# A four-layer fp32 transformer on one core: edge tokens in the first query block, more places for background pieces, and the last FFN kept for the tail

## The chip, the cores and the metric

The kernel runs on one core of a Trainium2 chip. A core has five engines with their own instruction queues: TensorE (PE, matmuls and transposes), VectorE (DVE), ScalarE (ACT), GpSimd (POOL) and SyncE (SP, which here issues the DMAs). The metric is the device time of one execution in microseconds; the time before is the median of three runs.

## The reference, cut to what matters

One sequence of 2048 tokens of width 128 goes through four layers, each an attention and an FFN with a residual sum around either (`x = x + f(layernorm(x))`), all in fp32:

- Layer 0: attention with 16 heads of width 8; FFN with an exact GELU.
- Layer 1: full attention with 16 heads of width 64 over all 2048 keys; FFN with 384 hidden columns and a SiLU gate.
- Layer 2: attention of every token to itself and its two neighbours in a ring (token 0 and token 2047 are neighbours); FFN with one of eight experts.
- Layer 3: a memory that is updated in 32 chunks of 64 tokens, each of which needs the state that the chunk before left; FFN with eight routed experts and a shared one, 176 hidden columns each.

```python
idx = jnp.stack([(i - 1) % s, i, (i + 1) % s], axis=1)      # layer 2: the ring
...
for c0 in range(0, S, CHUNK):                                # layer 3: 32 chunks in series
    g = _grad_fn(W_state, k[:, sl], v[:, sl]) * GRAD_SCALE
    ...
    (S_state, W_state), Wtraj = jax.lax.scan(step, (S_state, W_state), xs)
```

## The kernel before, in words

The kernel has three phases. Layer 0 runs first (0 to 906 us in the trace). Then layer 1's attention (`l1_attn`, 906 to 2595 us), with everything behind it as background work. Then the tail (`drain`, 2595 to 2999 us), in which the rest of that background work is done.

**Layer 1's attention.** The 2048 queries are cut into blocks of 512, 384, 512, 384 and 256 (`QB`: start, tokens, columns). A unit is one block with one pair of heads, so a block has eight units and the phase 40. A unit has 16 key steps of 128 keys. A key step issues four passes of score matmuls for the two heads (`ops`: high and low parts of keys and queries, and the negative row maximum), two exponentials on ACT, a few matmuls that look for the maxima of a later unit (`max_upto`, reduced by DVE into `mx`), the sums of the exponentials (`do_sum`, mostly on POOL) and the value matmuls of the step before (`do_pv`). After a unit, `u_end` divides by the sums, through DRAM, and after every second unit `stage_wo` multiplies by the output weights. With a block's last unit its tokens are added to `xs`, and `("x", qb)` is emitted: the block is ready for what follows.

**Edge tokens.** Background work runs in blocks of 256 tokens. Layer 2's attention of such a block (`stage_b`) needs a neighbour's keys and values on both sides. So that it needn't wait for the next query block, the attention of a few tokens (`EXTRA`) is computed as extra columns of one query block: tokens 1280, 1792 and 2047, in the second block, which has 388 columns instead of 384. `stage_m` takes these tokens through layer 1's FFN and writes their keys and values into `edge`. `stage_b` waits for `"m"`, and for the following block of 256 unless that block's first token is an extra one.

**Background.** For each block of 256 the stages are `stage_a` (layer 1's FFN), `stage_a2` (layer 2's projections), `stage_b`, `stage_b2` (layer 2's FFN), then for each 128 tokens `stage_c`, two times `chunk` (the recurrence of layer 3) and `stage_d`, and then `stage_g` (the router of the last FFN), `stage_e0`, the lanes `s_lane` (13 tiles of hidden columns for each block, 104 in all) and `stage_e1`. Each is a generator which yields wherever it would have to wait for another engine. What is yielded says what the next piece needs: a whole number asks for so many PSUM banks, `"T"` says that the piece has matmuls, a float is a delay.

**The planner.** The order on PE, DVE, ACT and POOL is written out when the program is built. `note` keeps an estimated clock for each engine. `fill` lets background pieces in: it goes through the helpers and parts in their order of priority and takes the first that `may` go, by its estimated ready time, by how far ACT and DVE are behind (`backlog`, `low`) and by free banks (`leave` banks are left alone), until the estimated PE clock has moved by a limit. With `only="t"` it takes only pieces that need no bank and aren't marked as having matmuls; since these leave the PE clock where it is, such a call takes all that are ready. In a key step of layer 1 there are two calls of `fill`, after the exponentials and maxima and after the value matmuls. The estimate can charge 0.12 us whenever the shape of the weights' tile on PE changes (`in0`); layer 0 is planned with that, layer 1 and the tail without.

PSUM has eight banks: three for scores (`st`), five (`mx`) for maxima, the value product and the background. In the tail all eight serve the background, and five more lanes take part.

Of the kernel before, what the change touches and what calls it, by code (L numbers as in the profile page):

```python
# [30 lines left out]
ATANH = (1.0000000039388743, 0.3333315796754013, 0.20012426861749952, 0.13980709417165652, 0.14087328632693624)  # L31
T = dict(lead0=22, more0=4, mgap=0.4, pvq=2, lim0=0.5, fq=(3,), pl=-0.5, pr=1.0, tlow=2, tback=3, late=0.3, pvp="mx", mxp="mx", ex=(1280, 1792, 2047), low=1, lows='ge', keep=1, leave=2, pvn=1, sp=0, rdy=40., eu=2, qg=(22, 16, 10), em=2, el=6, sem=0.2, same=1.2, tsame=3.0, order="hdmBbAaEcCeg", ps=dict(st=3, mx=5), dma=2.3, slack=0.1, lim=0.3, backlog=2.5, lead=(10, 8, 6), pp=7, dve=(14, 15), qp=(1, 1), lanes=2, xl=5,
         QB=[(0, 512, 512), (512, 384, 388), (896, 512, 512), (1408, 384, 384), (1792, 256, 256)])

# [36 lines left out]
def body(ctx: ExitStack, tc: tile.TileContext, x, pa, pb, pc, pi, pd, pr, pr0, pe, pw, out):  # L71
# [122 lines left out]
    class Part:  # L194
# [24 lines left out]
        def step(self):  # L219
            piece[0] = clk["T"]  # L220
            r = next(self.gen, "end")
            self.same = r == "same"
            self.ready = 0.0 if self.same else piece[0] + (r if type(r) is float else 0.0)
            self.pe = r == "T"
            self.banks = r if type(r) is int else 0
            self.seen = len(emitted) if r is False else -1
            if r == "end":
                emitted.add(self.key)
            return r != "end"
# [139 lines left out]
    xnd = dram.tile([128, S], F32, name="xnd")  # L369

    QB = T["QB"]
    EXTRA = T['ex']
    units = [(qb, p) for qb in range(len(QB)) for p in range(NP1)]
    qhh, qfs, kmx, mx1 = {}, {}, {}, {}

    qx = [mid.tile([128, 8], F32R, name=f"qx{i}") for i in range(2)]
    xq = {}

    def u_loadx(qb):
        t0, tn, n = QB[qb]  # L380
        xq[qb] = l1x.tile([128, 512], F32, name="xq", tag="xq", bufs=2)
        if n != tn:
            ge.memset(xq[qb][:, tn:n], 0.0)
            for i, t in enumerate(EXTRA):
                sy.dma_start(xq[qb][:, tn + i:tn + i + 1], xnd[:, t:t + 1])
        sy.dma_start(xq[qb][:, :tn], xnd[:, t0:t0 + tn])

    def u_qprep(u):
        qb, p = units[u]
        if qb not in xq:  # L390
            u_loadx(qb)
        n = QB[qb][2]
        yield 1
        ps = mi()
        mm(ps[:, :n], C("wq", p * 128, 128), xq[qb][:, :n])
        yield
        qf = l1x.tile([128, 512], F32, name="qf", tag="qf")
        se.activation(qf[:, :n], ps[:, :n], AF.Identity, bias=bq8[:, p:p + 1], scale=0.125)
        rel(ps)
        yield  # L400
        qhh[u] = l1q.tile([128, 512], F32R, name="qh", tag="qh")
        se.copy(qhh[u][:, :n], qf[:, :n])
        yield
        qfs[u] = qf
        tn, n = QB[qb][1:]
        if n > tn:
            for e in range(2):
                r = slice(64 * e, 64 * e + 64)
                se.copy(qx[u % 2][r, 4 * e:4 * e + n - tn], qf[r, tn:n])

# [14 lines left out]
    def u_max(u, i):  # L425

        qb, p = units[u]
        tn, n = QB[qb][1:]
        per = nmax(u) // 4
        c, r = divmod(i, per)  # L430
        qt, e = divmod(r, 2)
        if i == 0:
            mx1[u] = sm.tile([128, 2, 4, 4], F32, name="mx1", tag="mx1")
        if 128 * qt == tn:
            ps = amx()
            mm(ps[0:8], qx[u % 2], kmx[(u, c)])
            ve.tensor_reduce(mx1[u][0:8, 0, 3, c:c + 1], ps[0:8], AX.X, ALU.max)
            rel(ps)
            return 1
        pss = [amx() for _ in range(2)]  # L440
        for e in range(2):
            rows = slice(64 * e, 64 * e + 64)
            mm(pss[e], qhh[u][rows, qt * 128:(qt + 1) * 128], kmx[(u, c)][rows, :], par=e and 0.02)
        for e in range(2):
            ve.tensor_reduce(mx1[u][:, e, qt, c:c + 1], pss[e], AX.X, ALU.max)
            rel(pss[e])
        return 2

    def u_maxend(u):
# [6 lines left out]
        if n > tn:  # L456
            ve.tensor_reduce(m[0:8, 0, 3:4], mx[0:8, 0, 3, :], AX.X, ALU.max)
        yield 1
        t = mi()
        if n > tn:  # L460
            te.transpose(t[0:1, 256:264], m[0:8, 0, 3:4], ident[0:8, 0:8])
        for e in range(2):
# [4 lines left out]
        if n > tn:  # L467
            for e in range(2):
                se.mul(mbt[u % 2][64 * e:64 * e + 1, tn:n], t[0:1, 256 + 4 * e:256 + 4 * e + n - tn], -1.0)
        rel(t)  # L470
# [480 lines left out]
    psum_pools(**T["ps"])  # L951
    in0[0] = False
    leave[0] = T["leave"]
# [69 lines left out]
    def stage_wo(qb, part):  # L1023
# [4 lines left out]
        for p in range(2 * part, 2 * part + 2):  # L1028
            mm(ps[:, :n], C("wo", p * 128, 128), O.pop(p)[:, :n], start=(p % 2 == 0), stop=(p % 2 == 1))
            yield  # L1030
        if part == 0:
            w = l1w.tile([128, 512], F32, name="wac", tag="wac", bufs=1)
            se.activation(w[:, :n], ps[:, :n], AF.Identity, bias=bo1)
            rel(ps)
            wacc[qb] = w
            return
# [3 lines left out]
        if part < NP1 // 2 - 1:  # L1040
            return
        del wacc[qb]
        yield 1
        c0, nt = t0 // 128, tn // 128
# [8 lines left out]
        if n != tn:  # L1053
            ne = len(EXTRA)
            xm = edge_x[0] = sm.tile([ne, 128], F32, name="xm", tag="xm", bufs=1)
            for i, t in enumerate(EXTRA):
                sy.dma_start(xm[i:i + 1, :], xs[t % 128:t % 128 + 1, t // 128, :])
            yield 1
# [7 lines left out]
    def l1_attn():  # L1066
        LEAD = dict(zip((256, 384, 512), T["lead"]))
        LEAD.update({260: LEAD[384], 388: LEAD[512]})
        U = len(units)
# [66 lines left out]
        for g in range(16 * U):  # L1136
# [6 lines left out]
            if u + 2 < U:  # L1143
                if k == 1 and units[u + 2][1] == 0:
                    need(("q", u + 1))
                    u_loadx(units[u + 2][0])
                if k == T["qp"][n <= 256] and u + 2 >= EU:
                    helper(("q", u + 2), u_qprep(u + 2))
# [12 lines left out]
            for i, (a, b) in enumerate(ops):  # L1161
                for e in range(2):
                    rows = slice(64 * e, 64 * e + 64)
                    mm(pss[e][:, :n], a[rows], b[rows, :n], start=(i == 0), stop=(i == 3), par=e and 0.02)
            for e in range(2):
                pt = pp.tile([128, 512], F32, name="P", tag="P")
# [3 lines left out]
            max_upto(max_at(g + 16 + LEAD[n] + 1))  # L1170
            fill()
            if prev:
                do_sum(*prev[-1])
            if len(prev) == T["pvn"]:
                while prev:
                    do_pv(*prev.pop(0))
                fill()
            do_merge()
            prev.append((g, pts, v))
# [134 lines left out]
    def stage_m():  # L1314
# [21 lines left out]

        xt = sm.tile([128, 4], F32, name="xtm", tag="xtm", bufs=2)
        yield from norm_T(xt)
        h = sm.tile([128, 12], F32, name="hm", tag="hm", bufs=1)
        for k in range(3):  # L1340
# [3 lines left out]
            yield  # L1344
            th = sm.tile([128, 4], F32, name="thm", tag="thm", bufs=2)
            se.activation(th[:, :ne], ps[:, 0:ne], AF.Tanh, scale=0.5)
            yield
            ve.scalar_tensor_tensor(th[:, :ne], th[:, :ne], 1.0, ps[:, 0:ne], ALU.add, ALU.mult)
            ve.scalar_tensor_tensor(h[:, 4 * k:4 * k + ne], th[:, :ne], 0.5, ps[:, 64:64 + ne], ALU.mult, ALU.mult)
            rel(ps)  # L1350
            yield 1
        ps = mi()
        for k in range(3):
            mm(ps[:ne, :128], h[:, 4 * k:4 * k + ne], tok(wi, 6 + k), start=(k == 0), stop=(k == 2))
        yield
        ve.tensor_tensor(xm, xm, ps[:ne, :128], ALU.add)
        rel(ps)
        yield
        xt = sm.tile([128, 4], F32, name="xtm", tag="xtm", bufs=2)
        yield from norm_T(xt)  # L1360
        ps = mi()
        for i in range(2):
            mm(ps[:, 4 * i:4 * i + ne], tok(w2m, i), xt[:, :ne])
        yield
        for i in range(2):
            for j, t in enumerate(EXTRA):
                se.activation(edge[:, t // BN, i, int(t % BN > 0):int(t % BN > 0) + 1], ps[:, 4 * i + j:4 * i + j + 1],
                              AF.Identity, bias=b2m[:, i:i + 1])
# [257 lines left out]
    def chunk(b, c):  # L1626
# [48 lines left out]
        ve.scalar_tensor_tensor(u, tht, 2.0, u, ALU.mult, ALU.add)  # L1675
        yield
        mm(da, ef, w2)
# [320 lines left out]
    def s_e0():  # L1998
        for b in range(NB_):
            yield from wait(("g", b))  # L2000
            if b and not tail:
                yield from wait(("l", b - 1))
            yield from mark(("e0", b), stage_e0(b))
# [114 lines left out]
```

## Time and profile before

| what | us |
|---|---|
| median of three runs | 3005.0 (2992.95 to 3006.38) |
| profiled execution | 3001.08 |
| its span, first to last instruction | 2999.2 |
| layer 0 | 0 to 906 |
| layer 1's attention, 40 units | 906 to 2595 |
| tail | 2595 to 2999 |
| PE busy in these three | 816.8, 1608.5 (the five rows shown below), 344.3 |
| mean granted PE clock | 0.936 (0.76 in the tail) |

All instructions are recorded under the line of one helper, so the profile is read by tiles: `mi` is any PSUM tile, `P` the exponentials, `ka` keys and values, `km` keys for the maxima, `mx` the maxima, `acg` and `acd` the sums on POOL and on DVE, `xe` the input of the last FFN, `xst` the state of the recurrence, `acs` and `en` operands of a chunk's last matmuls. An fp32 matmul appears as two instructions.

### The profile page before, as it was taken

What the parts mean: (1) busy time and instruction counts of PE and PEld (TensorE: products, weight loads), DVE (VectorE), ACT (ScalarE), POOL (GpSimd) and SP (SyncE); (2) the same over time, 40 slices, a digit from 0 to 9 for tenths busy, and PEclk for the clock granted to TensorE, in tenths of its full rate; (3) what the DMA queues carried; (4) which work ended last, traced back from release to release, by engine and by line L of the source; (5) the groups of instructions that cost most, each with busy time, mean ns of one, the idle gap of its engine ahead of it and who ended that gap; (6) DMA issues with size and microseconds to landing.
All of it is one profiled execution on the core that took longest, in us unless ns stands there. A gap on an engine that the chain in (4) does not pass through costs nothing.

```text
span 2999.2 us, 49776 instructions
## 1 busy us (share of the span) xinstructions
PE 2769.9 (92%) x16719; PEld 1307.0 (44%) x16719; DVE 2194.9 (73%) x4699; ACT 1582.9 (53%) x3933; POOL 1522.3 (51%) x1762
## 2 busy tenths in 40 slices
PE   7999999999979899999999999899989898888998
PEld 2222222322234344454444444455544555565666
DVE  7899898898534666566666778887677769787765
ACT  1788887888854444444444444444434334333444
POOL 2400110201127688866776876677767556443444
PEclk9999999999979999999999999999999999776779
DMA  6311231321144333433442332233334343312244
GB/s 142 72 28 22 72 84 17 101 54 46 53 141 135 92 112 110 121 110 111 138 119 87 94 95 87 89 105 108 109 97 114 108 117 94 88 52 61 76 104 115
DMA packets 247749, 275.80 MB, mean 92 GB/s; under 512 B 95747, under 2 KB 183330, under 8 KB 247366
## 3 DMA queue, kind: packets, MB, share of 16 engines
q1 hardware_dynamic: 246630, 272.43, 33.2%
q8 instruction: 132, 2.16, 0.3%
q14 instruction: 123, 1.01, 0.1%
q10 hardware_dynamic: 864, 0.20, 0.0%
HBM read 229.97 MB, written 42.28 MB: 91 GB/s over the span
## 4 chain that ended last, share of the span: by engine, by line
PE 70%; DVE 18%; ACT 6%; issue 3%; DMA 3%; POOL 1%; SPq 0%; ACTq 0%; DVEq 0%; POOLq 0%
PE mi L147 70%; DVE mx L147 5%; ACT P L147 3%; DVE sB L147 1%; DVE o L147 1%; DVE gq L147 1%; DMA ka<-kvd 1%; DVE gt L147 1%; DVE xs L147 1%; ACT kf L147 1%; ACT kh L147 1%; DVE xn L147 1%; DVE sG L147 1%; DVE acd L147 1%; DVE sA L147 0%
## 5 line engine op out<-in xcount | busy, mean ns | idle before, releaser
L147 DVE TENSOR_REDUCE mx<-mi 128x1 f32<-128x512 f32 (+1 forms) x2080 | 1322.1, 683 | 582.8 <-PE mi L147 571.5
L147 ACT ACTIVATE P<-mi 128x512 f32<-128x512 f32 (+3 forms) x2304 | 1137.0, 551 | 1004.1 <-PE mi L147 973.2
L147 POOL TENSOR_TENSOR acg<-acg,P 128x512 f32<-128x512 f32 (+3 forms) x960 | 1011.4, 1083 | 181.8 <-ACT P L147 180.0
L147 PE MATMUL mi<-P,ka 128*64 128x512 f32 (+3 forms) x2560 | 597.6, 546 | 2.3 <-DVE mx L147 2.3
L147 PE MATMUL mi<-qh,ka 64*128 64x512 f32 (+3 forms) x2560 | 521.0, 406 | 9.7 <-DMA ka<-kvd 6.8
L147 PEld LDWEIGHTS mi<-qh,ka 64*128 64x128 f32 x2560 | 247.0, 189 | 382.5 <-issue 347.0
L147 PE MATMUL mi<-kop,qop 48*128 48x512 bf16 x1024 | 348.6, 405 | 24.5 <-DVE mx L147 12.1
L147 PE MATMUL mi<-qop,kop 50*128 50x512 bf16 x1024 | 317.8, 391 | 27.1 <-ACT P L147 24.7
L147 PE MATMUL mi<-P,vop 128*32 128x512 f32 x2048 | 304.3, 623 | 13.9 <-ACT P L147 13.9
L147 POOL TENSOR_SCALAR vep<-mv 128x2 f32<-128x2 f32 (+1 forms) x24 | 5.5, 229 | 495.6 <-DVE mv L147 495.6
L147 PE MATMUL mi<-km,qh 64*128 64x512 f32 x1024 | 225.6, 410 | 30.4 <-DVE mx L147 23.8
L147 PE MATMUL mi<-mbt,onr 64*128 64x512 f32 (+3 forms) x1280 | 228.7, 351 | 1.5 <-DMA mbt<-mb 1.5
L147 PE MATMUL mi<-ql,ka 64*128 64x512 f32 (+3 forms) x1280 | 229.2, 353 | 0.0
L147 PEld LDWEIGHTS mi<-P,ka 128*64 128x64 f32 x2560 | 129.2, 137 | 225.3 <-issue 195.1
L147 PEld LDWEIGHTS <-kop 50*128 50x128 bf16 x1024 | 63.6, 95 | 304.9 <-issue 281.6
L147 POOL TENSOR_TENSOR acg<-P 128x512 f32<-128x512 f32 (+3 forms) x80 | 91.1, 1158 | 202.5 <-DVE acd L147 162.0
L147 PEld LDWEIGHTS mi<-km,qh 64*128 64x128 f32 x1024 | 107.1, 189 | 60.5 <-DVE mx L147 38.5
L147 PEld LDWEIGHTS mi<-mbt,onr 64*128 64x128 f32 x1280 | 124.6, 190 | 13.9 <-DMA mbt<-mb 2.2
L147 PEld LDWEIGHTS mi<-ql,ka 64*128 64x128 f32 x1280 | 125.7, 192 | 0.0
L147 PEld LDWEIGHTS <-qop 48*128 48x128 bf16 x1024 | 72.9, 96 | 97.2 <-issue 82.7
L147 PEld LDWEIGHTS mi<-P,vop 128*32 128x32 f32 x2048 | 55.5, 109 | 119.8 <-issue 90.7
L147 POOL TENSOR_TENSOR kl<-kf,kh 128x512 f32<-128x512 f32 x32 | 40.9, 1278 | 110.9 <-ACT kh L147 82.4
(509 smaller groups left out, 3464.4 us busy)
## 6 DMA issues: line engine op xcount, KB each, us to landing
ka<-kvd SPq DMA_DIRECT2D x320, 384.0 KB
km<-khd SPq DMA_DIRECT2D x159, 256.0 KB
khd<-kh SPq DMA_DIRECT2D x32, 256.0 KB
kvd<-kh SPq DMA_DIRECT2D x32, 256.0 KB
kvd<-kl SPq DMA_DIRECT2D x32, 256.0 KB
kvd<-vt SPq DMA_DIRECT2D x16, 512.0 KB
ka<-in_pw_dram SPq DMA_DIRECT2D x37, 192.0 KB
w3s<-in_pw_dram SPq DMA_DIRECT2D x35, 192.0 KB
```

Source lines behind the costliest of these rows:

```text
L147: r = f(*a, **k)
```

## The change

1. `QB` becomes 384, 512, 512, 384, 256, and the first block carries five edge tokens (256, 768, 1280, 1792, 2047) in 392 columns. The order of the units is now a list of segments: two units of the second block, the eight of the first, the other six of the second, and then the rest as before. Query columns are loaded once for each segment. The rows of `xs` for the edge tokens are fetched before the first block is added to `xs`, since token 256 lies in that block.
2. In a key step `fill(9.0, "t")` is called after each of the first three score passes, after the first `fill`, after the value matmuls and after the second `fill`. A piece behind a float is now marked as having matmuls, and two plain yields ahead of matmuls (in `stage_wo` and `chunk`) become `"T"`.
3. `in0` stays true, so the charge for a change of tile shape holds in layer 1 and in the tail.
4. `s_e0` waits for the tail for every block, not for the FFN of the block before. `s_g` of a block waits for `e0` of the block before it, as it did.

```diff
+T = dict(ti=(0, 1, 2), tf=1, ... ex=(256, 768, 1280, 1792, 2047), ...
+         QB=[(0, 384, 392), (384, 512, 512), (896, 512, 512), (1408, 384, 384), (1792, 256, 256)])
...
-            self.pe = r == "T"
+            self.pe = r == "T" or type(r) is float
...
-    units = [(qb, p) for qb in range(len(QB)) for p in range(NP1)]
+    SEG = [(1, 0, 2), (0, 0, 8), (1, 2, 8), (2, 0, 8), (3, 0, 8), (4, 0, 8)]
+    units = [(qb, p) for qb, p0, p1 in SEG for p in range(p0, p1)]
+    seg = [i for i, (_, p0, p1) in enumerate(SEG) for _ in range(p0, p1)]
+    NX = 8
...
-    qx = [mid.tile([128, 8], F32R, name=f"qx{i}") for i in range(2)]
+    qx = [mid.tile([128, 2 * NX], F32R, name=f"qx{i}") for i in range(2)]
...
-            mm(ps[0:8], qx[u % 2], kmx[(u, c)])
-            ve.tensor_reduce(mx1[u][0:8, 0, 3, c:c + 1], ps[0:8], AX.X, ALU.max)
+            mm(ps[0:2 * NX], qx[u % 2], kmx[(u, c)])
+            ve.tensor_reduce(mx1[u][0:2 * NX, 0, 3, c:c + 1], ps[0:2 * NX], AX.X, ALU.max)
...
-    in0[0] = False
+    in0[0] = True
...
-            yield
+            yield "T" if p % 2 == 0 else 0
...
+        if n != tn:
+            ne = len(EXTRA)
+            xm = edge_x[0] = sm.tile([ne, 128], F32, name="xm", tag="xm", bufs=1)
+            for i, t in enumerate(EXTRA):
+                sy.dma_start(xm[i:i + 1, :], xs[t % 128:t % 128 + 1, t // 128, :])
+            piece[0] = clk["D"]
         yield 1
         c0, nt = t0 // 128, tn // 128
...
-                if k == 1 and units[u + 2][1] == 0:
+                if k == 1 and seg[u + 2] > seg[u + 1]:
                     need(("q", u + 1))
-                    u_loadx(units[u + 2][0])
+                    u_loadx(seg[u + 2])
...
                     mm(pss[e][:, :n], a[rows], b[rows, :n], start=(i == 0), stop=(i == 3), par=e and 0.02)
+                if T["tf"] and i in T["ti"]:
+                    fill(9.0, "t")
...
             fill()
+            if T["tf"]:
+                fill(9.0, "t")
             if prev:
                 do_sum(*prev[-1])
             if len(prev) == T["pvn"]:
                 while prev:
                     do_pv(*prev.pop(0))
+                    if T["tf"]:
+                        fill(9.0, "t")
                 fill()
+                if T["tf"]:
+                    fill(9.0, "t")
...
         ve.scalar_tensor_tensor(u, tht, 2.0, u, ALU.mult, ALU.add)
-        yield
+        yield "T"
         mm(da, ef, w2)
...
-            if b and not tail:
-                yield from wait(("l", b - 1))
+            while not tail:
+                yield False
             yield from mark(("e0", b), stage_e0(b))
```

## The prediction

> **What bounds the kernel now.** I read the page's slices first, then the same rows cut at the borders of the stages, which I took from the first score matmul (906.1 us), the last value matmul (2595.2 us) and the starts of units 8, 16, 24 and 32.
>
> ```profile
> PE 2769.9 (92%) x16719; PEld 1307.0 (44%) x16719; DVE 2194.9 (73%) x4699; ACT 1582.9 (53%) x3933; POOL 1522.3 (51%) x1762
> PEclk9999999999979999999999999999999999776779
> PE 70%; DVE 18%; ACT 6%; issue 3%; DMA 3%; POOL 1%; SPq 0%; ACTq 0%; DVEq 0%; POOLq 0%
> ```
>
> TensorE sets the time, but its granted clock falls to 0.6 to 0.7 in the last slices. By stage (columns: us, busy time and count of PE, weight loads, DVE, ACT, POOL; then clock and DMA):
>
> ```profile
> 906.00:1290.00 384.00, 373.62 (x2137) 164.08 (x2138) 229.07 (x356) 183.17 (x357) 302.69 (x268) 0.98 0.37 113
> 1290.00:1541.00 251.00, 246.21 (x1640) 125.69 (x1641) 158.72 (x291) 118.04 (x289) 183.73 (x187) 0.99 0.41 121
> 1541.00:1938.00 397.00, 377.62 (x2072) 169.93 (x2068) 307.99 (x557) 174.54 (x392) 289.64 (x250) 0.98 0.31 92
> 1938.00:2280.00 342.00, 326.22 (x2146) 171.78 (x2144) 246.17 (x520) 148.30 (x425) 235.78 (x273) 0.97 0.37 104
> 2280.00:2595.20 315.20, 285.17 (x2129) 163.78 (x2128) 244.73 (x611) 125.78 (x474) 191.63 (x292) 0.91 0.42 110
> 2595.20:2999.20 404.00, 344.26 (x1722) 256.50 (x1719) 289.18 (x1069) 160.07 (x659) 167.20 (x279) 0.76 0.31 79
> ```
>
> Up to 2280 us TensorE is full (95 to 98% busy, clock 0.97 or more): work pushed in there costs its own time. The tail after attention, 404 us, holds 344 us of PE at clock 0.76, so 344.26 x 0.76 = 262 us of work at full clock. That is the slack.
>
> Why is the tail long? The tile `acs` is used once in each of the 32 chunks of layer 3's recurrence (its matmul is two instructions):
>
> ```profile
> 1541.00:1938.00 397.00, 0.55 (x4) 0.39 (x4) 0.57 (x2) 0.98 0.31 92
> 1938.00:2280.00 342.00, 1.66 (x12) 1.16 (x12) 1.72 (x6) 0.97 0.37 104
> 2280.00:2595.20 315.20, 1.78 (x12) 1.29 (x12) 2.14 (x6) 0.91 0.42 110
> 2595.20:2999.20 404.00, 5.85 (x36) 4.43 (x36) 5.48 (x18) 0.76 0.31 79
> ```
>
> Only 14 chunks end during attention; 18 are left. They run in series from 2589 to 2924 us, 18.6 us each, and 75 us of last steps follow. The same view by `xe` shows no FFN product of layer 3 ahead of the tail (the 4 instructions before it are the router's): all 104 FFN tiles already run in the tail. So the tail is the chunk chain, with the FFN beside it.
>
> In attention a chunk ends every 28 to 35 us while they flow, with holes of 101 us (2060 to 2161) and 200 us (2207 to 2407) where the next block hasn't come. One chunk, in order of time:
>
> ```profile
> 1946.28 0.29 PE L147 MATMUL mi<-kf,xst 32*32 32x64 f32 x2
> 1949.23 0.20 ACT L147 ACTIVATE thf<-mi 32x64 f32<-32x64 f32 x1
> 1952.49 0.21 DVE L147 SCALAR_TENSOR_TENSOR af<-thf,mi 32x64 f32<-32x64 f32 x1
> 1961.47 0.17 DVE L147 SCALAR_TENSOR_TENSOR dzr<-u,mi 64x32 f32<-64x32 f32 x1
> 1962.37 0.54 POOL L147 TENSOR_TENSOR rr<-rr,mhalf 64x1 f32<-64x1 f32 x1 [0.98 <-DVE rr L147]
> 1968.43 1.01 DVE L147 TENSOR_SCALAR dz<-dzr,rr 64x32 f32<-64x32 f32 x1
> 1969.49 0.30 PE L147 MATMUL mi<-dz,kcs 64*64 64x32 f32 x2
> ```
>
> The steps last 0.2 to 1.0 us and the gaps 3 to 6 us: each piece waits for one of the two places of a key step (2.5 us) where background work is let in.
>
> **The change part by part.**
>
> *Edge tokens in the first block, run after units 0 and 1.* The small stage `m` needs the attention output of the edge tokens. Now they end with unit 15; its matmuls run at 1606 to 1651 us. After, they end with unit 9. Units 2 to 7 take (1246.8 - 999.1)/6 = 41.3 us, units 13 to 15 of 388 columns 34.3 us. Unit 9 then ends at 999 + 8 x 34.3 = 1273 us against 1541 us: stage `m`, and block 0 behind it, come some 270 us earlier. Tokens 256 and 768 are edges now, so blocks 0 and 2 need no successor; block 2 comes with unit 15 instead of unit 23, at about 1590 us instead of 1975 us. That closes the two holes. Cost: 2056 columns for 2052, over 8 units; the slope (41.3 - 34.3)/(512 - 388) = 0.056 us a column gives 1.8 us. The edge maxima keep their count (16 output rows for 8). DMAs: five column loads for three, a sixth load of a query block, five row loads for three at 0.51 us of SP's queue each. They stand in SP's queue beside the key loads, and the row loads are now ahead of the add to `xs`, which must wait for them. Now they issue at 704 to 888 us, so I take 3 us; if they come late, maxima are queued behind that add on DVE, and the worst DMA step of the chain (5.0 us, at 1560 us) bounds it at 5.
>
> *Pieces between score passes, after them and after the value matmuls.* No instruction is added. Pieces without matmul get up to five more places in a key step. Of the chunk's 23 us, the gaps before ACT, DVE and POOL steps are about 16; with one place per half microsecond I expect some 6. A chunk then takes 16 to 20 us with its start. ACT pieces now enter ahead of the step's exponentials, DVE pieces ahead of its maxima. The cover: a bank of scores is wanted again about 1.5 us after its scores end, and its exponential takes 0.55 us. Without that cover every late piece is PE idle time. Neither gain nor loss can be read from this trace: PE's waits for `mx` between 1290 and 2595 us are 36.2 us in all. If finer places empty half of it, -18; if they double it, +36. I take 0 here.
>
> *Tile changes in the planner's clock.* It sets only order. A key step of 512 columns is about 2.2 us by the planner without them and 2.44 with two changes at 0.12; the trace has 41.3/16 = 2.58. The planner comes nearer; counted inside the bounds above.
>
> *FFN in the tail only.* Nothing moves by itself, since all of it is there already. It keeps the early blocks from taking a PSUM bank and PE time in attention. The router step of blocks 1 to 7 moves to the tail (0.61 us of `xe` products, nothing).
>
> *The sum.* By attention's end I expect 24 to 26 chunks done. What leaves the tail: 12 chunks, 4 stages c, 5 d, about one b2. Without overlaps the tail's PE spends 39.9 us on 18 chunks, 30.0 on 7 c, 24.4 on 9 d, 12.8 on two b2: 26.6 + 17.1 + 13.6 + 6.4 = 64 us busy, 64 x 0.76 = 48 us at full clock. Attention must take these 48. Its price now: 40 units without background are 16 x 41.3 + 16 x 34.2 + 8 x 27 (extended along the slope) + 12 (the start) = 1435 us of 1689; the other 254 us carry background matmuls of 178 us at full clock, counted by tile: 1.43 us per us. So +48 (idle time takes the friction) to +69; I take +55, nearer the bare work because blocks 0 to 2 fall where the clock is 0.97 to 0.99.
>
> The tail. Chain of block 7, in today's times: last value matmul to the end of its b2 2595 to 2727 (132); stage c 26 (2795 to 2814 plus its norm); 4 chunks at 14.3, the mean of the last ten (57); last chunk to end 75. Sum 290. By PE: 344 - 64 = 280 us busy; at today's share and clock 280/0.852 = 329, at 90% and clock 0.9 280 x 0.76/0.9/0.9 = 263. I take 295, nearest the chain.
>
> Span: 906 + 1689 + 55 + 2 + 3 + 295 = 2950 us; with the 1.9 us that the profiled execution (3001.1) has around its span (2999.2): **2952 us**, 49 less than that execution and 53 less than the median 3005.
>
> *A rule against it.* DVE steps with two SBUF inputs are dearer in attention: `u` 1140 ns there, 219 in the tail; `dz` 850 and 398. Twelve chunks cost 12 x 1.4 = 17 us more of DVE, which is 70% busy there, so hidden. The Trainium skill ("SBUF — State Buffer", "Who interferes with whom") says that such a DVE instruction and a GpSimd one that reads SBUF block each other fully. The rows agree; by the rule alone, with every one of those 17 us ahead of a maximum that PE waits for, the time would be 2969 us.
>
> *And the clock.* From 2739.1 to 2793.7 us PE was busy 47.49 of 54.60 us at clock 0.50. The same skill ("TensorE: Matmul & The Clock Gate", "What's actually happening") has the full clock back after about 3.4 us of sustained work. By it a filled tail would take 263 us, the time 2920 us; the row says that 87% busy didn't bring it back, so I keep 295.
>
> **Rivals.**
> - *The tail shrinks to PE's floor, attention doesn't grow.* Finer places also take half of PE's `mx` waits: 906 + 1689 + 30 + 5 + 265 + 2 = 2897 us. For: 81 us of PE idle in attention. Against: full slices up to 2280 us. 0.27.
> - *Little moves.* Chunks stay at 30 us because PSUM banks, not places, hold them; about 18 done, tail 375, attention +22: 2999 us. For: the bank for the chunk's next product comes 7.7 us after its predecessor's end (1938.6 to 1946.3). 0.11.
> - *Slower: pieces ahead of the exponentials and maxima stall TensorE.* Place: key steps of units 10 to 39, 480 of them, above all those of 256 columns (315.2/128 = 2.46 us where the slope gives 1.7, at 78% DVE). At 0.1 us a step the gain of 49 is gone; at 0.2 it is 96: 3048 us. For: the multiply `o` at 971.9 us held DVE 10.8 us and PE idle 8.9. Against: ACT is 40 to 44% busy there. 0.15.
>
> The forecast itself holds 0.47. A measurement here tells 0.5% (15 us) from nothing. Faster than 2990: 0.47 + 0.27 less a little, 0.73; within: 0.11; slower: 0.16. The range runs from below the first rival to just short of the slower one's 3048: 2870 to 3035; the forecast's own is 2915 to 2990.
>
> **What would show it.** Stage `m` near 1330 us; 22 or more chunks ahead of the last value matmul and intervals under 22 us; attention 1710 to 1770 us long; tail 270 to 320 us with about 280 us of PE less its clock gain. Wrong if chunk intervals stay near 30 us, if PE's waits for `mx` or `P` double, or if attention grows by over 100 us.

## The result and the profile after

The changed kernel is slower. Its median is 3102.55 us (3082.65 to 3107.15) against 3004.75 us (2992.95 to 3006.38) before, a ratio of 1.032 with a 95% interval of 1.027 to 1.037. The profiled execution took 3082.65 us, 1.75 of them outside its span. First the page's busy times and the granted clock in 40 slices:

```profile
PE 2794.3 (91%) x16719; PEld 1311.3 (43%) x16719; DVE 2275.9 (74%) x4699; ACT 1602.3 (52%) x3942; POOL 1521.9 (49%) x1762
PEclk9999999999979999999889998999998999878888
```

The instruction counts of PE, DVE and POOL are the same as before, and ACT has 9 more. What stands out is the clock: before, it was low only in the last slices and once in layer 0; now there are dips from slice 20 on, in the middle of attention. (The chain that ended last was followed back over less than 1% of this span, so it says nothing here.)

By phase, and for three stretches within attention (columns: us, busy time and count of PE, weight loads, DVE, ACT, POOL, then clock and DMA):

```profile
903.20:2798.90 1895.70, 1747.76 (x10683) 876.32 (x10683) 1366.82 (x2807) 804.25 (x2213) 1236.85 (x1360) 0.93 0.33 96
2798.90:3080.90 282.00, 233.09 (x1155) 179.81 (x1152) 190.36 (x593) 124.87 (x387) 133.33 (x188) 0.85 0.45 113
1429.30:1505.60 76.30, 64.56 (x303) 30.34 (x302) 61.38 (x126) 26.02 (x90) 35.52 (x35) 0.78 0.22 62
1823.00:2026.00 203.00, 175.08 (x981) 84.31 (x980) 172.51 (x366) 77.75 (x249) 115.32 (x124) 0.92 0.23 68
2067.90:2238.10 170.20, 162.66 (x1020) 83.34 (x1018) 123.92 (x241) 75.08 (x172) 122.30 (x136) 0.98 0.35 104
```

The tail shrank from 404 us to 282 us, as hoped. Attention grew from 1689.1 to 1895.7 us: 207 us were paid for the 122 that were saved, and 3 came back in layer 0. (The two profiled executions lie 82 us apart, the medians 98.) The third row is unit 13 (one unit, 76.3 us) and the fourth units 20 to 22 (203 us for three). In both, DVE is 80 to 85% busy and the clock has dropped; in the fifth row, where no chunk runs, units take 37 to 48 us at 73% DVE and a clock of 0.98. So the price was paid in places, not in every key step.

The tile `acs` (two matmul instructions in each chunk) shows how much was moved:

```profile
903.20:2799.00 1895.80, 8.49 (x56) 6.24 (x56) 8.39 (x28) 0.93 0.33 96
2799.00:3080.90 281.90, 1.23 (x8) 0.91 (x8) 3.05 (x4) 0.85 0.45 113
```

28 chunks are now done in attention, where 14 were. They come in clumps: four that end from 1491.5 to 1555.3 us, eight from 1879.6 to 2034.2, eight from 2304.8 to 2455.6 and eight from 2669.4 to 2782.1, on average 20 us apart in a clump (16 to 22 by clump); four are left for the tail.

Inside a clump, in order of time (start, duration, instruction; in brackets the idle time before it and what ended it):

```profile
1867.81 0.54 POOL L147 TENSOR_TENSOR rr<-rr,mhalf 64x1 f32<-64x1 f32 x1 [3.74 <-DVE sA L147]
1867.91 5.47 DVE L147 TENSOR_SCALAR sB<-sA,pcs 128x128 f32<-128x128 f32 x1
...
1868.32 4.97 POOL L147 TENSOR_TENSOR acg<-acg,P 128x512 f32<-128x512 f32 x4
...
1875.27 0.23 DVE L147 TENSOR_SCALAR dz<-dzr,rr 64x32 f32<-64x32 f32 x1
...
1875.42 1.27 DVE L147 TENSOR_REDUCE mx<-mi 128x1 f32<-128x512 f32 x2
...
1876.15 0.79 PE L147 MATMUL mi<-km,qh 64*128 64x512 f32 x2 [3.66 <-DVE mx L147]
...
1880.08 0.49 POOL L147 TENSOR_TENSOR qab<-sC,ab 64x128 f32<-64x128 f32 x1 [6.78 <-DVE ab L147]
...
1880.26 5.32 DVE L147 TENSOR_TENSOR gq<-i,dO 32x64 f32<-32x64 f32 x1
...
1880.53 4.97 POOL L147 TENSOR_TENSOR acg<-acg,P 128x512 f32<-128x512 f32 x4
...
1885.83 1.27 DVE L147 TENSOR_REDUCE mx<-mi 128x1 f32<-128x512 f32 x2
...
1886.56 0.50 PE L147 MATMUL mi<-km,qh 64*128 64x512 f32 x1 [1.76 <-DVE mx L147]
```

Twice the same thing happens. A small background step on DVE (`sB`, `gq`) starts while POOL works on a small step of its own (`rr`, `qab`) and stays open for 5.3 to 5.5 us, within 0.1 us until the four running sums that POOL does next, back to back, are over. The maximum that stands behind it on DVE comes late, and the matmul that wants the maximum's bank leaves PE idle for 3.66 and 1.76 us. Between the two, with no sum running on POOL, `dz` takes 0.23 us; its mean in this attention is 1.29.

The groups of such steps on DVE in attention (busy us, mean ns of one):

```profile
L147 DVE TENSOR_TENSOR gq<-i,dO 32x64 f32<-32x64 f32 x14 | 38.3, 2735 | 0.2
L147 DVE TENSOR_SCALAR dz<-dzr,rr 64x32 f32<-64x32 f32 x28 | 36.2, 1293 | 3.8 <-POOL rr L147 3.6
L147 DVE SCALAR_TENSOR_TENSOR u<-tht,u 64x32 f32<-64x32 f32 x28 | 31.2, 1113 | 0.2
```

What PE waited for from 1270 to 2799 us (total, times, longest):

```profile
PE mi L147 <- DVE mx L147: 54.9, 26, 6.0
PE mi L147 <- DVE dz L147: 21.1, 8, 6.3
```

Before, the wait for `mx` was 36.2 us (25 times) and that for `dz` 1.4 us (twice). PE's idle time in attention went from 80 to 148 us, and the time at half clock from 116 to 270 us. Half clock loses half of its time, so of the 207 us idle time is 68 and the clock (270 - 116)/2 = 77; the other 62 are about the matmul work that moved in (busy time by clock: 1608.73 x 0.97 = 1560 us before, where the table ahead has 1608.5, and 1747.76 x 0.93 = 1625 after: 65 us).

### The profile page after: what moved, and what is told of

Its sections match the earlier page's. It is cut to its first block, busy times and chain, and to the rows that moved or that the text cites. A ratio compares the mean times of both kernels' runs of the same rounds, so it can differ in the third digit from the quotient of the medians.

```text
span 3080.9 us, 49745 instructions
## 1 busy us (share of the span) xinstructions
PE 2794.3 (91%) x16719; PEld 1311.3 (43%) x16719; DVE 2275.9 (74%) x4699; ACT 1602.3 (52%) x3942; POOL 1521.9 (49%) x1762
## 5 line engine op out<-in xcount | busy, mean ns | idle before, releaser
L147 PE MATMUL mi<-P,ka 128*64 128x512 f32 (+3 forms) x2560 | 621.9, 566 | 0.0
L147 PE MATMUL mi<-qh,ka 64*128 64x512 f32 (+3 forms) x2560 | 535.5, 416 | 3.5 <-DMA ka<-kvd 3.4
L147 PEld LDWEIGHTS mi<-qh,ka 64*128 64x128 f32 x2560 | 255.5, 195 | 361.1 <-issue 329.8
L147 PE MATMUL mi<-km,qh 64*128 64x512 f32 x1024 | 235.3, 422 | 45.3 <-DVE mx L147 35.6
```

The lines of the kernel that those rows point to most:

```text
L147: r = f(*a, **k)
```

## The experiments

The theory after this reading: the moved chunks' DVE steps are held by POOL's running sums, so that maxima come late, PE idles and its clock falls ("the held steps"). The rivals: DVE simply has too much to do; one of the four parts (blocks, places, charge, FFN) is at fault by its order alone; the moved matmul work costs what it costs. In the table, attention runs from the first score matmul to the last value matmul; PE's idle time, its time at half clock and DVE's busy time are those in attention. These come from one profiled execution of each kernel, which can lie off the median: after it is the shortest of four (3082.65 us), with "sums shared, after" and "sums halved" the longest. The ratio is to the kernel before on the same chip, so differences between two changed kernels are better read from the ratios.

| run | median us | ratio (95%) | attention | tail | chunks in attention | PE idle / half clock | DVE busy |
|---|---|---|---|---|---|---|---|
| before | 3004.75 | | 1689 | 404 | 14 | 80 / 116 | 1187 |
| after | 3102.55 | 1.032 (1.027 to 1.037) | 1896 | 282 | 28 | 148 / 270 | 1367 |
| places off | 3048.59 | 1.018 (1.013 to 1.022) | 1799 | 341 | 20 | 122 / 171 | 1273 |
| charge off | 3023.41 | 1.009 (1.005 to 1.012) | 1819 | 301 | 24 | 112 / 201 | 1340 |
| both off | 3032.49 | 1.012 (1.009 to 1.016) | 1768 | 361 | 16 | 117 / 188 | 1248 |
| old blocks | 3082.51 | 1.029 (1.026 to 1.033) | 1904 | 283 | 28 | 145 / 314 | 1355 |
| places alone, old blocks | 3034.79 | 1.012 (1.007 to 1.017) | 1823 | 309 | 23 | 117 / 236 | 1308 |
| short sums, after | 2902.01 | 0.965 (0.959 to 0.970) | 1695 | 285 | 28 | 48 / 65 | 1124 |
| short sums, before | 2915.34 | 0.969 (0.963 to 0.975) | 1601 | 410 | 14 | 33 / 31 | 1025 |
| short maxima, after | 3039.86 | 1.009 (1.006 to 1.013) | 1832 | 284 | 28 | 112 / 222 | 929 |
| short maxima, before | 2945.95 | 0.980 (0.976 to 0.984) | 1635 | 404 | 14 | 55 / 65 | 730 |
| POOL only writes, after | 2908.64 | 0.970 (0.967 to 0.974) | 1715 | 285 | 28 | 42 / 116 | 1134 |
| sums halved, after | 3191.27 | 1.060 (1.056 to 1.065) | 2016 | 285 | 28 | 222 / 399 | 1424 |
| sums shared, after | 3068.54 | 1.022 (1.019 to 1.026) | 1891 | 276 | 28 | 143 / 257 | 1491 |
| sums shared, before | 3017.89 | 1.005 (1.001 to 1.008) | 1686 | 421 | 13 | 80 / 96 | 1337 |
| steps off DVE, after | 3061.88 | 1.015 (1.010 to 1.020) | 1880 | 277 | 28 | 140 / 253 | 1252 |
| steps off DVE, charge off | 2993.70 | 0.995 (0.992 to 0.997) | 1791 | 284 | 23 | 99 / 191 | 1246 |
| steps off DVE, before | 3012.96 | 1.002 (0.999 to 1.004) | 1693 | 409 | 14 | 87 / 123 | 1114 |
| steps off DVE, places alone | 2992.79 | 0.993 (0.991 to 0.996) | 1792 | 293 | 23 | 106 / 174 | 1235 |

### Which part of the change

*Places off:* the extra calls of `fill` don't happen.

```diff
-T = dict(ti=(0, 1, 2), tf=1, ...
+T = dict(ti=(0, 1, 2), tf=0, ...
```

> The changed kernel without the finer places (the planner has 20 chunks done by the end of attention instead of 28). If pieces at the finer places hold up maxima and exponentials, attention falls from 1896 us to about 1730 us and the time to 2980 to 3010 us. If the price is DVE work under POOL's sums, attention falls only by the share of chunks that go back to the tail, 8 of the 14 moved, so to about 1780 us, and the time is 3030 to 3050 us. If the planner's charge for tile changes does the harm, the time stays within 15 us of 3102 us.

*Charge off:* the planner doesn't charge for tile changes in layer 1 and the tail.

```diff
-    in0[0] = True
+    in0[0] = False
```

> The changed kernel planned without the charge for tile changes in layer 1 and the tail (24 chunks by the end of attention). If the charge does the harm, by making PE look slower than it is and so letting pieces in before what they wait for is there, attention falls to 1700 to 1750 us and the time to 2950 to 2990 us. If the finer places do it, the time stays within 20 us of 3102 us. If the price is DVE work under POOL's sums, attention falls by 4 of the 14 moved chunks, 60 us, and the time is 3060 to 3080 us.

*Both off:* the two edits together, which leaves the blocks, the marks and the FFN in the tail.

> New blocks with edge tokens first and the FFN kept for the tail, but neither finer places nor the charge (16 chunks by the end of attention). All theories expect attention near the 1689 us of before plus the price of two chunks, 1690 to 1730 us, and a time from 2960 to 3005 us; if the new order of blocks is itself dear, over 3020 us.

*Old blocks:* the query blocks, edge tokens and order of units of before, with everything else of the change.

```diff
-T = dict(..., ex=(256, 768, 1280, 1792, 2047), ...
-         QB=[(0, 384, 392), (384, 512, 512), (896, 512, 512), (1408, 384, 384), (1792, 256, 256)])
+T = dict(..., ex=(1280, 1792, 2047), ...
+         QB=[(0, 512, 512), (512, 384, 388), (896, 512, 512), (1408, 384, 384), (1792, 256, 256)])
...
-    SEG = [(1, 0, 2), (0, 0, 8), (1, 2, 8), (2, 0, 8), (3, 0, 8), (4, 0, 8)]
+    SEG = [(i, 0, 8) for i in range(5)]
```

> Finer places, charge and FFN in the tail, but the blocks and edge tokens of before (28 chunks by the end of attention by the planner, all after unit 16). If the new order of blocks plays no part in the loss, attention is 1880 to 1930 us and the time 3080 to 3130 us. If edge tokens in the first block were to blame, attention is under 1780 us and the time under 3030 us.

*Places alone, old blocks:* the same with `in0` false.

> Blocks and edge tokens of before, no charge, but the finer places and the FFN kept for the tail. By the price that the runs show, some 13 us of attention for every chunk moved and 8 to 10 us back in the tail, a kernel with 20 to 24 chunks by the end of attention costs 3010 to 3040 us. If only the clumping of chunks under the charge were dear, it would be at or below the kernel before, 2960 to 3000 us.

No part is the culprit by itself, and none of the five runs is faster than before. The charge costs 0.6% without the new places (1.012 to 1.018) and 2.3% with them (1.009 to 1.032). The places cost 1.4% with the charge; without it they may even gain (1.012 to 1.009, intervals that overlap). The blocks hardly matter for the loss: without them it is 1.029. What the rows have in common is that each moves chunks into attention, and attention pays more than the tail gives back: after 207 for 122 us, charge off 130 for 103, both off 79 for 43, places alone 134 for 95. Per chunk moved, the full change pays 207/14 = 14.8 us and saves 122/14 = 8.7.

Chunks alone don't set the price, though: both off pays 79 us for only two of them. What is left in that kernel (blocks, marks, the FFN in the tail, and a second buffer for `wac` that the description of the change doesn't name; +1.2%) was not taken apart further. Three of the five runs fell where they were expected if the moved chunks are the price and the blocks play no part (places off, old blocks, places alone). Charge off came out at 3023 us, under the 3060 to 3080 expected from that and over the 2990 expected if the charge did the harm. Both off came out at 3032, where all theories expected at most 3005 and a time over 3020 was to speak against the new blocks. Old blocks acquits these only together with places and charge; whether they cost something by themselves no run shows.

### What makes attention pay

*Short sums, after and before:* POOL's running sum of the exponentials takes only the first 8 columns. The planner charges the full sum, so that the order on every engine stays what it was. The softmax sums of the other columns are left unfinished.

```diff
+                if self.n == 'P' and name == 'tensor_tensor' and tname(a[1]).startswith('acg'):
+                    r = f(*[v[:, :8] if hasattr(v, 'shape') else v for v in a], **k)
+                else:
+                    r = f(*a, **k)
```

> The changed kernel in its own order of instructions, but the 960 running sums on POOL take only the first 8 columns, which leaves the softmax sums of the other columns unfinished. POOL is then nearly free in attention. If attention got dear because DVE's steps wait for POOL's sums, attention falls from 1896 us to below 1780 us, and the distance to the kernel before with the same edit (e6) shrinks from 97 us to under 30 us. If DVE's own load or its order is the cause, both kernels gain about alike and the distance stays over 70 us.

> The kernel before with the same edit: POOL's running sums take 8 columns, the other sums are left unfinished. It gains where DVE waited for POOL: the multiplies by the reciprocal sums and the few chunks in attention. If waits for POOL are the price of background, attention falls by 40 to 70 us, half of what the changed kernel gains; if not, by less than 20 us in both.

*Short maxima, after and before:* layer 1's maxima are taken over 64 of the 512 columns, in the same order; the exponents are then less well centred.

```diff
+                if leave[0] and self.n == 'D' and name == 'tensor_reduce' and tname(a[1]).startswith('mi_'):
+                    r = f(a[0], a[1][:, :64], *a[2:], **k)
```

> The changed kernel in its own order, with POOL's sums whole again; in layer 1 each maximum is taken over the first 64 of its 512 columns, so the row maxima cover an eighth of the keys. DVE loses some 0.5 us for each of about 1000 maxima, 500 us of its 1367 us in attention. If DVE's load as such holds TensorE up, attention falls by 100 us or more, as far as with short sums or further. If it is the waiting of single small steps for POOL in the middle of chains that TensorE's queue stands behind, attention falls by less than 60 us.

> The kernel before with the same short maxima in layer 1. If DVE's load was the price of background already, attention falls by 40 us or more from 1689 us; if not, by less than 20 us.

Attention of the kernel with short sums, after, by stages as above:

```profile
903.30:2598.10 1694.80, 1646.91 (x10683) 833.60 (x10683) 1124.36 (x2807) 799.89 (x2213) 423.58 (x1360) 0.98 0.38 107
```

And with short sums, before:

```profile
903.90:2505.00 1601.10, 1568.49 (x10117) 778.14 (x10116) 1024.92 (x2332) 749.12 (x1932) 391.88 (x1269) 0.99 0.40 113
```

This turns the result round. With short sums the changed kernel is at 2902.01 us and the one before at 2915.34 (their ratios' intervals overlap; the profiled spans are 2883.3 and 2915.2 us): the 98 us of loss are gone, and there may be a small gain. DVE has the same 2807 instructions as in the changed kernel, yet is busy for 1124 us instead of 1367: 242 us of its "busy" time was waiting. Before, it was 1187 - 1025 = 162 us. The maxima tell the rival off as the cause of the difference: they free 1367 - 929 = 438 us of DVE in the changed kernel, nearly twice as much, and attention falls by only 64 us, against 54 before. That leaves 1832 - 1635 = 197 of the 207 us between the two kernels; with short sums it is 1695 - 1601 = 94. DVE's load isn't free: 64 is just over the 60 us expected at most without it, and 54 over the 40 expected with it. But it costs both kernels about the same.

Short sums also leave POOL idle, so it could still be POOL's load and not its reading.

*POOL only writes, after:* the sum takes 8 columns, and two memsets of 0.9 times its columns follow, so that POOL stays busy but reads next to nothing.

```diff
+                    r = f(*[v[:, :8] if hasattr(v, 'shape') else v for v in a], **k)
+                    for _ in range(2):
+                        self.e.memset(fillt[:, :9 * a[0].shape[1] // 10], 0.0)
```

> The changed kernel in its own order; each running sum on POOL takes 8 columns and is followed by two memsets of a scratch tile, 0.9 n columns each, so that POOL is busy about as long as with whole sums (the other columns' sums are left unfinished). The memsets only write. If DVE is held by POOL's reading of SBUF, attention is near the 1695 us of the short sums, under 1740 us, and DVE's u, dz and gq steps last 0.2 to 0.5 us. If it is enough that POOL is busy, because pieces of the chunk stand behind its sums in its queue, attention is near 1896 us, over 1840 us.

```profile
902.80:2617.70 1714.90, 1672.54 (x10683) 847.12 (x10683) 1134.48 (x2807) 800.99 (x2214) 1130.32 (x3280) 0.97 0.38 106
```

POOL is busy for 1130 us, nearly as long as in the changed kernel (1237), and attention takes 1715 us, not 1896: of the 201 us that short sums gave, 181 are there without making POOL idle, as expected if reading is the price (under 1740 us). The steps from above, in this kernel:

```profile
L152 DVE SCALAR_TENSOR_TENSOR u<-tht,u 64x32 f32<-64x32 f32 x28 | 4.8, 172 | 0.0
L152 DVE TENSOR_TENSOR gq<-i,dO 32x64 f32<-32x64 f32 x14 | 4.7, 334 | 0.2
L152 DVE TENSOR_SCALAR dz<-dzr,rr 64x32 f32<-64x32 f32 x28 | 10.5, 375 | 6.4 <-POOL rr L152 6.3
```

`u` takes 172 ns instead of 1113 and `gq` 334 instead of 2735. But a memset here is shorter (0.29 to 0.48 us) than a sum (1.30 us at 512 columns), so a step that waits for one POOL instruction would wait less.

*Sums halved, after:* each running sum is issued as two of half the width. What is read stays the same, each instruction is shorter.

```diff
+                    h = a[0].shape[1] // 2
+                    for cs in (slice(0, h), slice(h, 2 * h)):
+                        r = f(*[v[:, cs] if hasattr(v, 'shape') else v for v in a], **k)
```

> The changed kernel, complete computation, in its own order, with each running sum on POOL as two instructions of half the columns. If it is the length of a POOL instruction that DVE's steps wait out, the steps u, dz and gq get a third to a half shorter and attention falls by 40 to 100 us to under 1860 us. If POOL's reading holds DVE whatever the length, because the next sum follows at once, attention stays at 1880 to 1960 us (POOL has some 15% more to do) and the steps keep their lengths.

```profile
905.70:2921.30 2015.60, 1793.16 (x10683) 896.72 (x10683) 1423.66 (x2807) 804.70 (x2214) 1369.11 (x2320) 0.90 0.32 90
```

Attention gets longer still, 2016 us. Groups of this kernel in attention:

```profile
L152 DVE TENSOR_TENSOR gq<-i,dO 32x64 f32<-32x64 f32 x14 | 30.9, 2206 | 0.2
L152 DVE SCALAR_TENSOR_TENSOR u<-tht,u 64x32 f32<-64x32 f32 x28 | 34.6, 1236 | 1.0 <-POOL u L152 1.0
L152 DVE TENSOR_TENSOR o<-o,rb 128x392 f32<-128x392 f32 x8 | 48.1, 6017 | 8.1 <-DMA rb<-rcd 4.8 <-ACT P L152 3.3
```

A half sum lasts 0.74 us at 256 columns, and `u` still takes 1.24 us and `gq` 2.2; the large multiply `o` of the unit's end takes 6.0 us, where it took 1.43 in the changed kernel. Shorter POOL instructions don't free the steps. With the run before it this says that it is mainly the reading, not the length of the instruction or POOL's load, that holds them; reads as short as the memsets weren't tried. Attention of 1880 to 1960 us was expected for that. Why it is longer still, by 120 us in the profiled executions and by some 85 us of the whole time by the ratios (1.060 against 1.032), isn't settled: POOL's sums themselves are 14% longer in all (two of 741 ns for one of 1301).

### Ways around it

*Sums shared, after and before:* six of 16 key steps have their sums on DVE instead of two.

```diff
-dve=(14, 15)
+dve=(4, 5, 9, 10, 14, 15)
```

> The changed kernel with key steps 4, 5, 9, 10, 14 and 15 summed on DVE instead of 14 and 15 alone: 8 of 28 sums of a unit go from POOL (1.08 us) to DVE (0.6 us). Complete computation. If POOL's hold on the port is the price, attention falls by 30 to 80 us although DVE has 150 us more to do, and the time is 3020 to 3070 us. If DVE's load is the price, the time rises over 3120 us.

> The kernel before with the same split of the sums, complete computation. If POOL's hold on the port costs it too (88 us with short sums), the time falls by 10 to 40 us to 2960 to 2995 us, ahead of both kernels. If DVE's load decides, it rises over 3015 us.

POOL falls from 1237 to 953 us in the changed kernel, DVE rises from 1367 to 1491, and attention in the profiled executions is the same within 5 us in both kernels (1891 for 1896, 1686 for 1689). By the ratios the changed kernel gains about 1% (1.032 to 1.022; 3068.54 us lies just within the 3020 to 3070 expected if POOL's reading is the price, but attention was to fall by 30 to 80), and the kernel before loses 0.5%. Most of what POOL reads less, DVE pays for by having more to do.

*Steps off DVE, four runs:* the held steps of the chunk and its neighbours go to other engines: `u`, the last multiply of `h` and, in attention, the norm's `xn` to POOL, `dz` and `gq` to ACT. The third run is the kernel before with this and with the last FFN kept for the tail; the fourth is "places alone, old blocks" with this.

```diff
-        eng = eng or ve
+        eng = eng or (ve if tail else ge)
...
-            ve.tensor_tensor(g1[r, :, k:k + 32], i1[r].unsqueeze(1).to_broadcast([r.stop - r.start, BC3, 32]),
-                             last(t)[r].to_broadcast([r.stop - r.start, BC3, 32]), ALU.mult)
+            for c in range(BC3):
+                se.mul(g1[r, c, k:k + 32], i1[r], t[r, c, CH - 1:CH])
...
-        ve.scalar_tensor_tensor(u, tht, 2.0, u, ALU.mult, ALU.add)
+        ge.tensor_tensor(u, u, at, ALU.add)
...
-        ve.tensor_scalar(dzn[:, 0, :], dz, rr[:, 3:4], 0.025, ALU.mult, ALU.mult)
+        se.mul(dzn[:, 0, :], dz, rr[:, 3:4])
...
-        ve.scalar_tensor_tensor(th, h2, 0.5, d["ab"], ALU.mult, ALU.mult)
+        ge.tensor_tensor(th, h2, d["ab"], ALU.mult)
```

> The changed kernel, complete computation, with the steps u, hth and (in attention) the normalisation xn on POOL and dz and gq on ACT instead of DVE; constants are folded elsewhere. These steps hold DVE 174 us in attention and would need about 55 us without waiting. If they are the price, attention falls by 70 to 130 us to about 1790 us and the time to 2980 to 3040 us. If the contention as a whole is (POOL gets more work that reads SBUF), attention stays over 1860 us and the time over 3070 us.

> The same edit on the changed kernel without the charge for tile changes (3023 us). If the steps are the price, it gains 60 to 100 us, to 2925 to 2965 us, ahead of both kernels. If not, it stays over 3005 us.

> The same edit on the kernel before, with its last FFN kept for the tail as in the change. Half as many chunks run in attention, so it gains half as much: 20 to 50 us, to 2955 to 2985 us, if the steps are the price; nothing or a loss, 2995 to 3020 us, if not.

> The same edit with the blocks of before, no charge, the finer places and the FFN in the tail (e10, 3035 us). If the steps are the price, it gains 60 to 100 us, to 2935 to 2975 us; if not, it stays over 3015 us.

I had expected 60 to 130 us from this and got less: attention falls by 16 us in the changed kernel (1896 to 1880), by 28 with the charge off (1819 to 1791) and by 31 for places alone (1823 to 1792). The ratios fall by 1.7, 1.4 and 1.9%, some 42 to 57 us of the whole time. DVE is relieved by 115, 94 and 73 us, but `dE` (879 ns in the last of the four), `o` and others are still held. So these steps carry part of the price, and DVE's held time isn't paid one for one: 115 us less of it gave 16 us of attention. Where the rest sits (other held steps, or the moved ones now standing behind the sums in POOL's queue) no run shows. Still, two of the four are ahead of both kernels, if by less than 1%: 2993.70 us (0.995) and 2992.79 us (0.993). Attention and tail of the latter:

```profile
902.40:2694.10 1791.70, 1685.79 (x10512) 844.39 (x10512) 1235.25 (x2521) 811.35 (x2212) 1296.06 (x1455) 0.95 0.36 101
2694.10:2987.10 293.00, 250.50 (x1327) 188.93 (x1323) 199.76 (x674) 135.41 (x469) 148.72 (x235) 0.87 0.43 108
```

It pays 1792 - 1689 = 103 us in attention for 404 - 293 = 111 in the tail: the balance has just turned. The kernel before gains nothing by the same edit (1.002), so keeping the FFN for the tail costs nothing that can be measured, unless the two parts of that edit cancel.

## Why the prediction was wrong

The forecast was 2952 us; the changed kernel takes 3102.55. By its steps:

- **Stage `m`: right; "that closes the two holes": wrong.** `m`'s matmuls run at 1318 to 1339 us, where "near 1330" was forecast. But from the last chunk of a clump to the first end of the next it is 324, 271 and 214 us. Four, eight, eight, eight and four chunks are the blocks of 256 tokens that the five query blocks complete, and the first chunk of each of the four clumps in attention ends 207 to 265 us after the last unit of its query block: a clump comes only after that, which edge tokens don't change. (The reading of the trace before had left out a third hole, 2441 to 2531 us, and that the last four chunks ahead of the tail already end 17 to 23 us apart. Its border at 1290 us isn't the start of unit 8, which is 1246.8; no sum rests on it.)
- **Finer places: right in what they do, wrong in what they cost.** A chunk in flow takes 20 us on average (16 to 20 forecast) and 28 are done by the end of attention (24 to 26). Their cost was taken as 0 between -18 and +36 us on PE's wait for `mx`. That wait grew by 19 us and the one for `dz` by 20, together about the upper bound; the time at half clock that came with them was in no bound.
- **The charge for tile changes: wrong.** "The planner comes nearer; counted inside the bounds above" stood for 2.3% (1.009 to 1.032, some 70 us) once the places are there. Why the charge does that was not taken apart; the rows show only that with it more chunks go into attention, 28 instead of 24.
- **The tail: right in the sum, by luck.** 295 forecast, 282 measured. The chain behind it had 132 + 26 + 57 = 215 us up to the end of the last chunk and 75 after it. It took 156 (2798.9 to 2954.7) and 126: 59 less and 51 more. With the chunks early, the FFN is what is left over. The rows by `xe` from the last chunk to the end, before and after, have 144 and 236 of its 444 matmul instructions in the tail:

```profile
2924.20:2999.20 75.00, 37.37 (x144) 25.60 (x144) 0.37 (x1) 0.93 0.49 115
2954.70:3080.90 126.20, 63.21 (x236) 42.29 (x236) 1.09 (x3) 0.88 0.57 128
```

- **The price in attention: this is the step that failed.** "1.43 us per us" for 48 us of moved work gave +55, between +48 and +69; it was +207. The moved work was 65 us, and 344.26 x 0.76 - 233.09 x 0.85 = 64 by the tail, so 16 or 17 too small, with the two to four more chunks in it; the price was 207/65 = 3.2 us per us. The runs with short sums split it. There, attention grows from 1601 to 1695 us, 94 us for 1646.91 x 0.98 - 1568.49 x 0.99 = 61 us of moved work: 1.5 us per us. (That this is near the 1.43 proves little, since 1.43 was taken with whole sums, and the forecast itself used 55/48 = 1.15.) The other 113 us are the running sums' doing: they cost 1896 - 1695 = 201 us of attention after, and 1689 - 1601 = 88 us before.
- **"12 x 1.4 = 17 us more of DVE, which is 70% busy there, so hidden": the term inside it.** It was mis-sized and not hidden. The waiting inside DVE instructions rose by 242 - 162 = 80 us, not 17: `u` and `dz` make up 33 of it (25.9 + 28.3 us longer than with short sums after, 12.9 + 8.3 before), and `xn` (20), `gq` (18), `hth` (12), `sB` (11) and `dE` (6) add theirs, while `o` waits 14 us less than before. And a mean of 70% hid nothing: in the clumps DVE is at 80 to 85%, with the maxima in its queue behind the held step, and PE behind the maxima.

The rule that the prediction weighed and set aside spoke to the point. The Trainium skill ("SBUF — State Buffer", "Who interferes with whom") has a DVE instruction with two SBUF inputs contend with a GpSimd one that reads SBUF, and not with one that only writes. The run in which POOL only writes agrees (`u` 1113 to 172 ns). Where the page and the trace differ is the length: the page ("Summary: rules for kernel authors") has the second one to issue wait until the first finishes, and `gq`, which issued 0.18 us after `qab` on POOL, waited here through that and through four sums. The prediction also counts `dz` among the steps with two SBUF inputs; it is a `tensor_scalar` of one tensor and a factor for each partition, and it was held too (1293 ns, 282 with short sums).

Of the rivals, the slower one had the mechanism's outer half: maxima late on DVE, PE idle, 3048 us. But it put the cause in the order of the pieces, spread at 0.1 to 0.2 us over 480 key steps; it was held DVE instructions, in the clumps. Its argument against ("ACT is 40 to 44% busy there") looked at the wrong engine. The floor rival's tail came about as near as the forecast's (265 against 282 measured), and its attention failed as the forecast's did.

The prediction's closing test named the right sign: "if attention grows by over 100 us". It grew by 207.

## What to carry to other kernels

Before work is moved under a phase that PE fills, look at the moved steps' durations in that phase and in the one they come from: a step that is two to five times longer there (`dz` 850 against 398 ns, `u` 1140 against 219) isn't sure to be hidden by a mean load of 70%, because what stands behind it in the queue waits too, as the maxima did here. A mean busy share doesn't tell work from waiting inside an instruction; shrinking the other engine's reads without touching the order does, in one run (here 242 of DVE's 1367 us were waiting). Two edits to a planner that moved the time by -0.4% and +0.6% one by one cost +2.0% together, so such edits are best tried in all four combinations.

## What was not expected of the hardware

- A held DVE step doesn't get its turn after one POOL instruction. `gq` stayed open for 5.32 us, over the rest of `qab` and four sums back to back, `sB` for 5.47 us over the rest of `rr` and four sums. The sums weren't slowed: four in 4.97 us is 1.24 us each.
- Cutting the sums in two, which would give a waiting step twice as many turns, made the kernel 6.0% slower than before (1.056 to 1.065), and `o` at 392 columns went from 1.43 to 6.02 us.
- Steps with one SBUF input are held as well: `sB` (a `tensor_scalar`) above, and the copy `dE`, 771 ns in the changed kernel and 159 with short sums. With POOL only writing, `dE` is at 285 and `dz` at 375 ns (282 with short sums), so these seem to be held a little by writes too, while `u` is not (172, and 188 with short sums).
- The clock took as much again as the waits did: 68 us more of idle time came with 154 us more at half clock, worth 77. No run sets the one without the other, and their ratio varies: 42 us idle with 116 at half clock where POOL only writes, 55 with 65 with short maxima in the kernel before.
